# First-layer softmax sums turned and added up by VectorE instead of summed by TensorE

## The chip, the cores and the metric

The kernel runs on one core of one Trainium2 chip. A core has five engines that run side by side, each with its own queue: TensorE (PE in the profile; its weight loads are shown as PEld), VectorE (DVE), ScalarE (ACT), GpSimd (POOL) and SyncE (SP, which here issues DMA transfers). TensorE writes its results into PSUM, which holds eight banks of 128 partitions by 512 numbers of four bytes. The metric is the time of one execution on the device, in microseconds (us), as a median of several runs.

## The reference

Two layers of attention over images. The input x holds 8 images of 32 x 32 places with 512 channels. Each layer takes a group norm (32 groups of 16 channels), projects queries, keys and values, takes a softmax over the 1024 places of the image, multiplies by the values, projects the result, and adds it to x.

```python
# layer 0: 16 heads of 32 channels
qkv = xt @ w_qkv
attn = softmax(einsum('bhid,bhjd->bhij', q * 32 ** -0.5, k))
out = einsum('bhij,bhjd->bhid', attn, v) @ w_proj + b_proj
# layer 1: 4 heads of 128 channels, with relative positions
scores = (q @ k) / sqrt(128) + position_logits(q)
out = (softmax(scores) @ v) @ Wo
```

All of it is computed in four-byte floating point.

## The kernel before

**Layout.** An image is held with channels on the partitions, in four blocks of 128 channels by 1024 places. Scores are computed turned round: keys on the partitions, queries along the row. The softmax leaves out the subtraction of the maximum (a check of all sums at the end chooses a general path if that was not safe), so a head needs exp of the scores, the product of exp with the values, the sum of exp over the keys, and a division.

**The first layer's attention** (`attention_0`) works in steps. A step is named by (m, h, j): m is one of four blocks of four heads, h one of two halves of the queries (512), j one of eight blocks of 128 keys. `front` makes the scores of four heads (line 727) in the four-bank PSUM tile `ps` and lets ScalarE take exp (line 742) into one of the three slots of `e_room`, each 128 x 2048. `back`, one step later, multiplies by the values into the PSUM bank `acc` (line 753) and lets VectorE add the exp tile onto the first one of its group (line 765), so that after the eight steps of a group (m, h) one slot holds, for each of four heads, 128 partial sums for each query. Two slots take turns for exp; the third holds the running sum. When a new group begins, the slot of its first exp becomes the sum, and the old sum's slot joins the turn, so the exp of the third step of the new group writes over the old sum.

**The end of a group** (`finish`): four matmuls with a matrix of ones (line 775) add up the 128 partitions of each head's part and spread the sum over that head's 32 partitions, in the bank `acc`. `normalise` (lines 667 to 708) copies that to memory (ScalarE), turns it by blocks of 32 x 32 (VectorE, line 669), takes a reciprocal of 16 numbers per partition, notes the largest sum for the check, spreads the reciprocals back (line 704), and GpSimd multiplies the result q[m] by them (line 708).

**The second layer's attention** (`attention_1`) ends its groups in another way: `added_up` (lines 676 and 677) turns the 128 x 512 partial sums on VectorE and adds up blocks of 32, leaving 16 numbers per partition, and one small matmul with the constant matrix `fold` (line 895) adds the four partition groups and spreads the result.

**Projections** are 2 x 2 block products with seven multiplications (`seven`, line 341 by way of `by_columns`): products are summed into three PSUM tiles x, y and z, in the order x, y, x, y, z, y, z. VectorE reads the half-done y twice (`a`, line 431, and `b`, line 439), and the next product into y must wait for that. The tiles x, y, z come from the three banks tagged `bank`. Those banks also serve the second layer's scores and sums and the position logits (`pp`). The names in a profile carry the matrix: y_wo is the y of the output projection Wo of the second layer, y_q and y_k those of queries and keys, y_wp that of the first layer's projection.

**What sets the order.** A recording layer schedules the instructions when the program is built. The order on each engine is then fixed, and every engine works through its own queue; `issue_after` orders an instruction behind a given one on its engine. The Python generators set which work lies beside which: in image loop b, `side_by_side` draws the first layer's attention of image b step by step and spreads beside it the work of other images: the first layer's projection Wp of image b-1 (`after_0`), Wo of image b-2 woven with the group norm of image b-1 (`after_1`, `norm_1`), the second layer's projections with the position logits (`second`), the whole second attention of image b-1 between two steps, and the first layer's projections of image b+1. Every yield of `attention_0` counted as one step before. In loop 0 `attention_first` also draws the second unit of the value products. SyncE's queue carries weight slices, image blocks and outputs.

Of the kernel before, what the change touches and what calls it, by code (L numbers as in the profile page):

```python
# [9 lines left out]
F32 = mybir.dt.float32  # L10
# [17 lines left out]
def quick_path(  # L28
# [305 lines left out]

    added = [None]

    def by_columns(out, weights, moving, start, stop, open_sum=False):

        for g in range(P // 32):
            columns = slice(32 * g, 32 * g + 32)  # L340
            ins = nc.tensor.matmul(  # L341
                out[columns, :],
                weights[:, columns],
                moving,
                start=start,
                stop=stop,
                skip_group_check=open_sum,
            )
            if in_place[0]:
                tc.keep_in_program_order(ins)  # L350
        in_place[0] = False
# [65 lines left out]
    def seven(fs, u, rows, sink, name, hook=None):  # L417

        product = taken(fs, u, rows)
        x = bank(f"x_{name}")
        product(x, 0, True)
        p1 = snapshot("e1", f"p1_{name}")
        nc.scalar.copy(p1, x)
        yield HC
        y = bank(f"y_{name}")
        product(y, 5, True)
        a = snapshot("es1", f"a_{name}")  # L430
        reader[0] = begun[0] = nc.vector.tensor_add(a, y, p1)
        sink.early(p1, a)
        yield HC
        product(x, 1, False)
        sink.c11(x)
        yield HC
        product(y, 4, False)
        b = snapshot("es1", f"b_{name}")
        reader[0] = half_done[0] = nc.vector.tensor_add(b, y, p1)
        sink.middle(b)  # L440
        yield HC
        z = bank(f"z_{name}")
        product(z, 6, True)
        p7 = snapshot("e1", f"p7_{name}")
        nc.scalar.copy(p7, z)  # L445
        yield HC
        product(y, 2, False)
        sink.c12(y, p1)
        if hook is not None:
            hook()  # L450
        yield HC
        product(z, 3, False)
        sink.c21(z, a)
        sink.c22(b, p7)
        yield HC
# [14 lines left out]
    def five_last(fs, u, sink, name, p1):  # L470
        product = taken(fs, u, False)
        y = bank(f"y_{name}")
        product(y, 5, True)
        a = snapshot("es1", f"a_{name}")
        reader[0] = begun[0] = nc.vector.tensor_add(a, y, p1)
        sink.early(p1, a)
        yield HC
        product(y, 4, False)
        b = snapshot("es1", f"b_{name}")
        reader[0] = half_done[0] = nc.vector.tensor_add(b, y, p1)  # L480
        sink.middle(b)
        yield HC
        z = bank(f"z_{name}")
        product(z, 6, True)
        p7 = snapshot("e1", f"p7_{name}")
        nc.scalar.copy(p7, z)
        yield HC
        product(y, 2, False)
        sink.c12(y, p1)
        yield HC  # L490
        product(z, 3, False)
        sink.c21(z, a)
        sink.c22(b, p7)
        yield HC
# [75 lines left out]
    class Plain:  # L570
# [15 lines left out]
            nc.vector.tensor_add(self.dst[1][0], self.shape(y), self.shape(p1))  # L586

        def c21(self, z, a):
            nc.vector.tensor_add(self.dst[0][1], self.shape(z), self.shape(a))

        def c22(self, b, p7):
            s = self.shape
# [68 lines left out]
    def normalise(dst, acc_sums, name, engine=nc.gpsimd):  # L661

        su = mem.tile([P, NB], F32, tag="rec", name=f"su_{name}", bufs=2)
        nc.scalar.copy(su, acc_sums)
        turned = mem.tile([P, NB], F32, tag="rec", name=f"tu_{name}", bufs=2)
        nc.vector.transpose(turned, su)
        few = turned.rearrange("p (t c) -> p t c", c=32)[:, :, 0]  # L670
        multiply(dst, few, few, su, name, engine)

    def added_up(out, esum, name):

        turned = mem.tile([P, NB], F32, tag="rec", name=f"tu_{name}", bufs=2)
        nc.vector.transpose(turned, esum)
        nc.vector.tensor_reduce(
            out, turned.rearrange("p (t c) -> p t c", c=32), axis=AX.X, op=ALU.add
        )

    def few_tile(name, n=1):
        return mem.tile([P, n, NB // 32], F32, tag=f"few{n}", name=name, bufs=3 if n == 1 else 1)
# [31 lines left out]
    def attention_0(q, k, v, b, blocks=range(NT)):  # L714

        steps = [(m, h, j) for m in (0, 2, 1, 3) for h in range(NH) for j in blocks]
        state = {}

        def front(m, h, j):
            name = f"0_{b}_{m}_{h}_{j}"  # L720
            ps = psum.tile([P, HB, NB], F32, tag="ps", name=f"ps_{name}", bufs=1)
            for i in range(2):

                some = slice(64 * i, 64 * i + 64)
                for r in range(HB):
                    rows = slice(r * D0, (r + 1) * D0)
                    nc.tensor.matmul(  # L727
                        ps[some, r, :],
                        k[m][rows, j * P + 64 * i : j * P + 64 * i + 64],
                        q[m][rows, h * NB : (h + 1) * NB],  # L730
                        start=True,
                        stop=True,
                    )
            at = turn.pop(0)
            if j == blocks[0]:

                turn.append(sum_at[0])
                sum_at[0] = at
            else:
                turn.append(at)  # L740
            e = e_room[:, at]
            nc.scalar.activation(e, ps, AF.Exp, scale=D0 ** -0.5)  # L742
            return e

        def back(m, h, j, e):
            name = f"0_{b}_{m}_{h}_{j}"
            if j == blocks[0]:
                state["acc"] = psum.tile([P, NB], F32, tag="acc", name=f"acc_{name}", bufs=1)
                state["first"] = e
            acc = state["acc"]  # L750
            for r in range(HB):
                c0 = (m * HB + r) * D0
                nc.tensor.matmul(  # L753
                    acc[r * D0 : (r + 1) * D0, :],
                    v[:, j, c0 : c0 + D0],
                    e[:, r, :],
                    start=(j == blocks[0]),
                    stop=(j == blocks[-1]),
                )
            if j == blocks[1]:  # L760
                state["esum"] = state["first"]
            if j != blocks[0]:

                with tc.issue_after(reader[0].ins) if beside_norm[0] else nullcontext():
                    summed[0] = nc.vector.tensor_add(state["esum"], state["esum"], e)  # L765
            if j != blocks[-1]:
                return
            nc.scalar.copy(q[m][:, h * NB : (h + 1) * NB], acc)
            state["ended"] = (m, h, state["esum"])

        def finish(m, h, esum):
            name = f"0_{b}_{m}_{h}"
            su = psum.tile([P, NB], F32, tag="acc", name=f"sums_{name}", bufs=1)
            for r in range(HB):
                nc.tensor.matmul(
                    su[r * D0 : (r + 1) * D0, :],
                    ones,
                    esum[:, r, :],
                    start=True,
                    stop=True,  # L780
                )
            normalise(q[m][:, h * NB : (h + 1) * NB], su, name)

        pending = None
        for at in steps:
            if "ended" in state:
                finish(*state.pop("ended"))
            e = front(*at)
            if pending is not None:
                back(*pending)  # L790
            pending = (*at, e)
            yield 2
        back(*pending)
        yield 1
        finish(*state.pop("ended"))

    def position_logits(q, posT, b):

# [203 lines left out]
    def attention_first(st):  # L1002

        values = project_rows(st["xn"], WV0, st["v"], "v0_0", units=(1,))
        steps = attention_0(st["q"], st["k"], st["v"], 0, [0, 1, 4, 5, 2, 3, 6, 7])
        for at, cost in enumerate(steps):
            if at < NT // 2:
                for _ in range(2):
                    next(values, None)
            yield cost  # L1010
# [152 lines left out]
    def side_by_side(first, rest, total, alone=0):  # L1163


        steps = CC * NH * NT + 1 - alone
        done = 0
        at = -alone
        for _ in first:
            at += 1  # L1170
            while done * steps < total * at:
                cost = next(rest, None)
                if cost is None:
                    done = total * steps
                    break
                done += cost
        run(rest)
# [629 lines left out]
```

## Time and profile before

| what | us |
|---|---|
| median of 3 runs (3792.39 to 3792.98) | 3792.49 |
| the profiled execution | 3792.3 |
| its span, first to last instruction | 3790.5 |
| PE busy | 3764.2 (99%) |
| DVE busy | 2579.9 (68%) |
| ACT busy | 1689.2 (45%) |
| POOL busy | 651.4 (17%) |
| sums with ones, line 775, PE | 71.4 |
| e_room additions, line 765, DVE | 1074.6 (448 of 2399 ns) |
| granted TensorE clock | 0.999 of full |

In a row of groups stand the line, the engine, the operation, what is written and read by the program's names, the sizes and the count; then the busy time in us and the mean time of one in ns; then how long the engine stood idle just before, and what ended most of that. Busy time counts overlapping instructions once. Most matrix products appear as two records, and those of different column groups overlap, so 512 records of 596 ns are busy for only 71.4 us. A row of a timeline gives the start in us, the time from the first start to the last end in us, the instructions, and in brackets the idle time before and what ended it.

### The profile page before, as it was taken

To read this page: it belongs to the slowest core of one execution; us is meant where nothing else is said; L and a number is where in the kernel's file an instruction comes from. 1 tells how busy PE (TensorE), PEld (TensorE's weight loads), DVE (VectorE), ACT (ScalarE), POOL (GpSimd) and SP (SyncE) were. 2 spreads that over 40 slices of the span, in tenths; PEclk is the share of its full clock that TensorE was granted. 3 is DMA by queue.
4 is the path that set the end of the run, shared out by engine and by line. 5 is a ranking of instruction groups with operands and counts; after the bars stand their busy time and mean duration, and the time that the engine had idled before them with its cause. 6 is when DMAs were issued, how large, how long until landed. Compare 5 with 4: busy or idle time off the path is not lost. (4 is left out here: it accounts for less than half of the span.)

```text
span 3790.5 us, 79715 instructions
## 1 busy us (share of the span) xinstructions
PE 3764.2 (99%) x34478; PEld 1367.7 (36%) x34478; DVE 2579.9 (68%) x2974; ACT 1689.2 (45%) x1705; POOL 651.4 (17%) x397
## 2 busy tenths in 40 slices
PE   9999999999999999999999999999999999999998
PEld 4232244322443234432343323433234332334353
DVE  6778675686756867569665696656866569765555
ACT  3555543445434454344534445344453445553132
POOL 1342101131001310013101131011310113001201
PEclk9999999999999999999999999999999999999999
DMA  6122120232202312023120241103411033110321
GB/s 187 64 106 69 39 57 10 72 102 54 56 12 93 85 48 56 16 92 93 38 56 18 94 96 39 48 22 99 91 40 42 25 99 78 29 43 29 104 50 26
DMA packets 482982, 234.71 MB, mean 62 GB/s; under 512 B 269600, under 2 KB 461376, under 8 KB 481600
## 3 DMA queue, kind: packets, MB, share of 16 engines
q1 hardware_dynamic: 470992, 213.74, 20.6%
q0 software_dynamic: 2608, 13.70, 1.0%
q8 instruction: 273, 4.47, 0.5%
q10 hardware_dynamic: 9024, 2.10, 0.3%
q14 instruction: 85, 0.70, 0.1%
HBM read 170.72 MB, written 58.72 MB: 61 GB/s over the span
## 5 line engine op out<-in xcount | busy, mean ns | idle before, releaser
L765 DVE TENSOR_TENSOR e_room<-e_room 128x2048 f32<-128x2048 f32 x448 | 1074.6, 2399 | 403.3 <-ACT e_room L742 400.1
L742 ACT ACTIVATE e_room<-ps 128x2048 f32<-128x2048 f32 x512 | 961.9, 1879 | 788.6 <-PE ps L727 752.5
L853 ACT ACTIVATE e<-ps 128x512 f32<-128x512 f32 x512 | 306.0, 598 | 634.8 <-PE ps L851 594.2
L727 PE MATMUL ps<-q,k 32*64 32x512 f32 x8192 | 575.5, 613 | 0.2 <-ACT e_room L742 0.2
L753 PE MATMUL acc<-e_room,v 128*32 128x512 f32 x4096 | 551.0, 604 | 0.0
L850 PE MATMUL ps<-q,k 128*128 128x512 f32 x1024 | 529.6, 599 | 0.2 <-DVE posT L836 0.2
L862 PE MATMUL acc<-e,v 128*128 128x512 f32 x1024 | 521.8, 592 | 0.0
L873 DVE TENSOR_TENSOR es<-es,e 128x512 f32<-128x512 f32 x384 | 301.1, 784 | 292.8 <-ACT e L853 288.5
L708 POOL TENSOR_TENSOR q<-q,su 128x512 f32<-128x512 f32 x127 | 190.6, 1501 | 1488.1 <-DVE su L704 1443.6
L851 PE MATMUL ps<-posT,sel 128*128 128x512 f32 x512 | 406.7, 794 | 0.0
L850 PEld LDWEIGHTS ps<-q,k 128*128 128x128 f32 x1024 | 188.2, 190 | 225.1 <-issue 217.3
L727 PEld LDWEIGHTS ps<-q,k 32*64 32x64 f32 x8192 | 120.0, 129 | 389.1 <-issue 216.5
L862 PEld LDWEIGHTS acc<-e,v 128*128 128x128 f32 x1024 | 193.1, 189 | 146.8 <-issue 105.2
L753 PEld LDWEIGHTS acc<-e_room,v 128*32 128x32 f32 x4096 | 81.9, 108 | 411.4 <-issue 364.1
L851 PEld LDWEIGHTS ps<-posT,sel 128*128 128x128 f32 x512 | 97.3, 190 | 122.5 <-issue 122.5
L836 DVE TENSOR_TENSOR posT<-pp,posT 32x512 fp32r<-32x512 f32 x128 | 111.8, 874 | 31.9 <-ACT posT L831 30.6
L593 POOL TENSOR_TENSOR k<-b_k,p_k 128x512 f32<-128x512 f32 x32 | 50.4, 1574 | 478.3 <-ACT p_k L445 467.6
L593 POOL TENSOR_TENSOR v<-b_v,p_v 128x512 f32<-128x512 f32 x32 | 51.5, 1609 | 436.4 <-ACT p_v L445 430.9
L831 ACT CAST posT<-pp 32x512 fp32r<-32x512 f32 x128 | 105.7, 826 | 46.0 <-PE pp L818 44.9
L593 POOL TENSOR_TENSOR q<-b_q,p_q 128x512 f32<-128x512 f32 x32 | 67.6, 2112 | 260.7 <-ACT p_q L445 260.7
L341 PE MATMUL y_v<-w_v,f_xn 128*32 128x256 f32 x1536 | 100.8, 381 | 0.0
L341 PE MATMUL y_k<-f_xn,w_k 128*32 128x512 f32 x768 | 100.7, 594 | 0.0
(223 smaller groups left out, 4384.0 us busy)
## 6 DMA issues: line engine op xcount, KB each, us to landing
w_qkv<-ws_qkv SPq DMA_DIRECT2D x168, 128.0 KB, 2.4
d<-x0T SPq DMA_DIRECT2D x32, 512.0 KB, 3.1
x1T<-d SPq DMA_DIRECT2D x32, 512.0 KB, 5.4
d<-x1T SPq DMA_DIRECT2D x32, 512.0 KB, 3.6
x2T<-d SPq DMA_DIRECT2D x32, 512.0 KB, 6.2
w_qkv<-in_L_conv_w_qkv SPq DMA_DIRECT2D x126, 128.0 KB, 2.2
out<-ot SPq DMA_DIRECT2D x240, 64.0 KB, 2.0
xs<-in_x SPq DMA_DIRECT2D x224, 64.0 KB, 2.5
```

Of the source, the lines that this page charges most:

```text
L341: ins = nc.tensor.matmul(out[columns, :], weights[:, columns], moving, start=start, stop=stop, skip_group_check=open_sum,)
L593: nc.gpsimd.tensor_tensor(self.dst[1][1], s(b), s(p7), op=ALU.add)
L708: engine.tensor_tensor(dst, dst, su, op=ALU.mult)
L727: nc.tensor.matmul(ps[some, r, :], k[m][rows, j * P + 64 * i : j * P + 64 * i + 64], q[m][rows, h * NB : (h + 1) * NB], start=True, stop=True,
L742: nc.scalar.activation(e, ps, AF.Exp, scale=D0 ** -0.5)
L753: nc.tensor.matmul(acc[r * D0 : (r + 1) * D0, :], v[:, j, c0 : c0 + D0], e[:, r, :], start=(j == blocks[0]), stop=(j == blocks[-1]),)
L765: summed[0] = nc.vector.tensor_add(state["esum"], state["esum"], e)
L850: nc.tensor.matmul(ps, k[h][:, keys], q[:, h, queries], start=True, stop=False)
L851: nc.tensor.matmul(ps, sel_flat[:, keys], posT[:, h, queries], start=False, stop=True)
L853: nc.scalar.activation(e, ps, AF.Exp, scale=1.0 / math.sqrt(D1))
L862: nc.tensor.matmul(acc, v[:, j, h * D1 : (h + 1) * D1], e, start=(j == 0), stop=(j == NT - 1),)
L873: added[0] = nc.vector.tensor_add(state["esum"], state["esum"], e)
```

## The change

The group end of the first layer takes the second layer's way, for all groups of an image but the last. `finish` becomes a generator. It is created at the end of the step in which the group's last `back` ran. In the second half of that step VectorE turns and adds up heads 0 and 1 (`added_up`), in the second half of the next step heads 2 and 3. After two more half-step calls four small matmuls with `fold` combine them in a bank tagged `bank`, and `normalise_few` does the rest; it has no copy by ScalarE and no turning. The last group of each image keeps the matmuls with ones and `normalise`.

The turns are ordered behind `calm[0]`: the last recorded VectorE instruction that read a half-done y (`a` or `b`), or a Plain output from z (`c21`). `attention_0` now yields twice per step, each for half of a step, and `side_by_side` counts by half; `attention_first` draws its value products at every second yield.

```diff
-        reader[0] = begun[0] = nc.vector.tensor_add(a, y, p1)
+        reader[0] = begun[0] = calm[0] = nc.vector.tensor_add(a, y, p1)
...
-        reader[0] = half_done[0] = nc.vector.tensor_add(b, y, p1)
+        reader[0] = half_done[0] = calm[0] = nc.vector.tensor_add(b, y, p1)
...
-            nc.vector.tensor_add(self.dst[0][1], self.shape(z), self.shape(a))
+            calm[0] = nc.vector.tensor_add(self.dst[0][1], self.shape(z), self.shape(a))
...
         def finish(m, h, esum):
             name = f"0_{b}_{m}_{h}"
-            su = psum.tile([P, NB], F32, tag="acc", name=f"sums_{name}", bufs=1)
+            dst = q[m][:, h * NB : (h + 1) * NB]
+            if (m, h) == steps[-1][:2]:
+                su = psum.tile([P, NB], F32, tag="acc", name=f"sums_{name}", bufs=1)
+                for r in range(HB):
+                    nc.tensor.matmul(
+                        su[r * D0 : (r + 1) * D0, :], ones, esum[:, r, :], start=True, stop=True
+                    )
+                normalise(dst, su, name)
+                return
+            few = few_tile(f"fw_{name}", HB)
+            for r in range(HB):
+                if r % 2 == 0:
+                    yield
+                with tc.issue_after(calm[0].ins):
+                    added_up(few[:, r, :], esum[:, r, :], f"{name}_{r}")
+            yield
+            yield
+            su = bank(f"sums_{name}")[:, : NB // 32]
             for r in range(HB):
                 nc.tensor.matmul(
-                    su[r * D0 : (r + 1) * D0, :],
-                    ones,
-                    esum[:, r, :],
-                    start=True,
-                    stop=True,
+                    su[r * D0 : (r + 1) * D0, :], fold[:, 0, :], few[:, r, :], start=True, stop=True
                 )
-            normalise(q[m][:, h * NB : (h + 1) * NB], su, name)
+            normalise_few(dst, su, name)
 
         pending = None
+        ending = iter(())
         for at in steps:
-            if "ended" in state:
-                finish(*state.pop("ended"))
             e = front(*at)
             if pending is not None:
                 back(*pending)
             pending = (*at, e)
-            yield 2
+            if "ended" in state:
+                ending = finish(*state.pop("ended"))
+                next(ending)
+            yield 1
+            next(ending, None)
+            yield 1
         back(*pending)
-        yield 1
-        finish(*state.pop("ended"))
+        yield 2
+        run(finish(*state.pop("ended")))
...
-            if at < NT // 2:
+            if at < NT and at % 2:
...
-        for _ in first:
-            at += 1
+        for cost in first:
+            at += cost / 2
```

More of the change, by code (lines that the diff above doesn't have):

```diff
@@ L335, in quick_path @@
     added = [None]
+    calm = [None]
     def by_columns(out, weights, moving, start, stop, open_sum=False):
@@ L474, in five_last @@
         a = snapshot("es1", f"a_{name}")
-        reader[0] = begun[0] = nc.vector.tensor_add(a, y, p1)
+        reader[0] = begun[0] = calm[0] = nc.vector.tensor_add(a, y, p1)
         sink.early(p1, a)
@@ L479, in five_last @@
         b = snapshot("es1", f"b_{name}")
-        reader[0] = half_done[0] = nc.vector.tensor_add(b, y, p1)
+        reader[0] = half_done[0] = calm[0] = nc.vector.tensor_add(b, y, p1)
         sink.middle(b)
```

## The prediction

> **What bounds the kernel now.** I read the page's busy times first, then the groups of instructions by line, the waits, the stage windows, and last the timelines of the stretch that the windows point at.
>
> The page's first part, and TensorE's own entry in the table of waits (longest in total, times, longest):
>
> ```profile
> PE 3764.2 (99%) x34478; PEld 1367.7 (36%) x34478; DVE 2579.9 (68%) x2974; ACT 1689.2 (45%) x1705; POOL 651.4 (17%) x397
> ...
> PE y_q L341 <- DVE a_q L431: 0.6, 1, 0.6
> ```
>
> TensorE (PE) is busy 99% of the span, and no engine keeps it waiting for long. What leaves TensorE shortens the program, as long as nothing new makes it wait. VectorE (DVE) has 32% free on average. The groups that the change touches or resembles:
>
> ```profile
> L775 PE MATMUL sums<-e_room,ones 128*32 128x512 f32 x512 | 71.4, 596 | 2.4 <-ACT q L768 2.0 <-DVE e_room L765 0.4
> L669 DVE STREAM_TRANSPOSE tu<-su 128x512 f32<-128x512 f32 x64 | 45.2, 706 | 54.4 <-ACT su L667 51.4 <-POOL q L708 2.9
> L676 DVE STREAM_TRANSPOSE tu<-es 128x512 f32<-128x512 f32 x64 | 45.1, 705 | 1.7
> L677 DVE TENSOR_REDUCE fw<-tu 128x16 f32<-128x512 f32 x64 | 43.8, 684 | 2.0
> L895 PE MATMUL sums<-fw,fold 128*128 128x16 f32 x128 | 19.5, 227 | 0.0
> ```
>
> The average hides where VectorE is full. Windows of 10 us (columns: length, PE, weight loads, DVE, ACT, POOL busy, clock, DMA share, GB/s), in image loop 3:
>
> ```profile
> 1270.00:1280.00 10.00, 10.00 (x108) 2.50 (x104) 9.90 (x17) 5.31 (x6) 2.12 (x2) 1.00 0.45 164
> ...
> 1310.00:1320.00 10.00, 10.00 (x108) 2.60 (x104) 9.86 (x13) 4.94 (x4) 3.27 (x2) 1.00 0.51 115
> 1320.00:1330.00 10.00, 9.89 (x104) 2.24 (x96) 8.89 (x9) 4.34 (x3) 0.00 (x0) 1.00 0.60 117
> 1330.00:1340.00 10.00, 10.00 (x116) 2.57 (x112) 6.55 (x5) 4.80 (x4) 1.95 (x1) 1.00 0.51 97
> ```
>
> From 1263 to 1325 VectorE is busy 60.8 of 62 us. The same stretch comes back near 800, 1730, 2200 and 2660, longer near 3130, and shorter near 340. It is where Wp's, the norm's and Wo's element work falls beside the first layer's first two groups. Its end, in the timelines of PE and DVE:
>
> ```profile
> 1270.92 1.05 PE L775 MATMUL sums<-e_room,ones 128*32 128x512 f32 x8
> 1271.90 1.11 PE L727 MATMUL ps<-q,k 32*64 32x512 f32 x16
> ...
> 1322.55 1.90 PE L341 MATMUL x_q<-x1T,w_q 128*32 128x512 f32 x16
> 1324.56 1.92 PE L341 MATMUL y_q<-f_xn,w_q 128*32 128x512 f32 x16
> ...
> 1321.66 2.24 DVE L765 TENSOR_TENSOR e_room<-e_room 128x2048 f32<-128x2048 f32 x1
> 1323.83 0.67 DVE L431 TENSOR_TENSOR a_q<-y_q,p_q 128x512 f32<-128x512 f32 x1
> 1324.43 2.27 DVE L765 TENSOR_TENSOR e_room<-e_room 128x2048 f32<-128x2048 f32 x1
> ```
>
> A set of 16 product records takes 1.72 us start to start, so the y_q product was due at 1324.27. It starts at 1324.56, after a_q, which reads the bank it adds to: VectorE's slack is already used up there. The sums take 0.98 us of TensorE (1270.92 to 1271.90).
>
> [...] a_q sits behind an e_room addition while its operands have long been there, and TensorE stops.
>
> **The change, part by part.** 56 of 64 finishes change, seven per image.
>
> *TensorE, removed:* 56 x 0.98 = 54.9 us. *Added:* eight fold records of 16 columns in four column groups. In the second layer a fold's two records take 0.14 us to the next matmul (1503.97 to 1504.11), which then takes 0.08 longer: 0.22 is the low end. Eight weight loads of 110 ns, none hidden, give 0.9. I take 0.3, near the low end, because the eight sums loads now cover one another (14.1 us busy in all, where 512 x 109 ns would be 56). [...] Net -0.68 each, -38.1 us if nothing waits.
>
> *ScalarE, removed:* 56 copies of 0.59 us. They lie beside TensorE's products; removing them is worth only the 2.0 us that sums waited for L768.
>
> *VectorE, added:* four transposes and four reductions per finish. Three transposes in a row take 1.88 us (1296.54), so 0.63 each; an operation of 0.69 lets the next start after 0.60, so a reduction takes 0.60. 4 x 0.63 + 4 x 0.60 = 4.92. *Removed:* one transpose, 0.63. Net +4.3, x 56 = 240 us: VectorE goes to about 2820 us, 74%. Most of it is covered by TensorE's products; not in the stretch.
>
> *The stretch.* By the built order of the changed kernel, between a_wp of the second unit and a_q, both groups' eight transposes and reductions each stand ahead of a_q, all other VectorE work is the same, and one reciprocal chain (1315.02 to 1316.04, 1.02 us) moves behind a_q. Nothing queued there can be skipped. So a_q moves by 2 x 4.92 - (0.62 + 0.71) for the old transposes - 1.02 - 0.59 idle used up (0.28 and 0.31, at 1282.98 and 1291.68) = +6.9 us, and TensorE waits for it: first at the wo products' a_wo and its banks, in all until the y_q product. TensorE's own saving of 1.4 us vanishes into that wait. +6.9 for each of image loops 2 to 6. In loop 7 both chains stay ahead of a_q: 9.84 - 1.43 - 1.47 idle = +7.0, then -1.0 for the third finish. In loop 1 only one group falls in: 4.92 - 0.62 - 0.87 idle = 3.4 at a_q, less 0.9 of slack, +2.6.
>
> *Two lighter places.* Group (2,1) ends beside a position stage (1395 to 1407, VectorE nearly full): exp must wait for the last transpose, and the fold takes the bank of z_k, whose reader stands behind an e_room addition. Following the queue by hand from 1395.68, with 4.92 added and the old chain's 1.86 taken off, TensorE waits 0.3 + 0.3 + 1.0 us: +0.8 net. Group (1,0) ends just ahead of the second layer's attention (1442): v's readers move 1.9 us and hold its first score bank, then its third e: waits of 1.4 and 0.8, +1.0 net. Both in loops 1 to 6. If VectorE has more slack than I see, both are -0.7; if less, twice as much.
>
> *Elsewhere* (groups (2,0), (1,1), (3,0)) VectorE is 50 to 70% busy; after the final e_room addition it has no addition to make for one step, and eight instructions fit. -0.68 each. The e_room slot must be free by the exp of the third step; the last transpose is some 1.5 us ahead of it there.
>
> *Moved:* reciprocal, check, spread and POOL's multiplication come about two steps later; POOL idled 1444 us ahead of it, and the output is read a group later at the earliest. SP's queue has five block loads one place later: covered by DMA queues busy about a fifth of the time; uncovered, some 2 us each. The first image's value products and the half counts issue the same work half a step later: nothing.
>
> *Sum against the profiled 3792.3 us (span 3790.5):* loop 0: 7 x -0.68, +2.5 for stretches at 94 to 96% (70 to 90, 150 to 160) = -2.3. Loop 1: +2.6 + 1.8 - 4 x 0.68 = +1.7. Loops 2 to 6: 6.9 + 0.8 + 1.0 - 3 x 0.68 = +6.7, x 5 = 33.5. Loop 7: 7.0 - 1.0 - 0.5 = +5.5. In all +38: 3830 us. The runs' median, 3792.49, is the profiled time within 0.2.
>
> **The rivals.**
> *VectorE's work hides (faster).* Over the whole span it fits: 240 us into 1210 idle. Then 38 + 2 us come off: 3752. It decides from the point where a_q is no later than 1324.3 less TensorE's lead; against it, the queue order and the stall already there. 0.08.
> *The two sides cancel.* If only the six stretches cost (about 41 us) and all 44 others gain 0.68 (-30), with a fold at 0.22 or VectorE's instructions a tenth cheaper: 3792 to 3800. 0.06 for within 0.2%.
> *The fold's bank becomes a second bound.* A fold takes one of three banks from its start to VectorE's check. If that costs 1 us at half of the 44 finishes outside the stretch beyond what I count, 3850 to 3860. For it: both ends hang on a full queue. Against it: in the light places the bank was free for several products. 0.12.
> That the change doesn't do what it says is excluded by the built order: 448 transposes and reductions on VectorE, 224 fold matmuls on TensorE.
>
> **How the numbers follow.** Forecast 0.74, bank 0.12, faster 0.08, same 0.06. A difference of 0.2% (7.6 us) is about what a measurement of this kernel can tell from none. Slower 0.86. Range: low end the stretches alone with little loss elsewhere, 3798; high end the forecast with the lighter places doubled and half the bank rival, 3856.
>
> **What would show it.** Right: PE idle before L341 and at the stretch's ends released by DVE a_wo, a_q and x2T, near 8 us per stretch; windows there with PE at 85 to 90% and DVE at 97% or more; the period between such stretches growing from 467 to about 474 us; elsewhere PE at 100%. Wrong: PE still 100% in the stretches (faster), or waits at the folds or score matmuls outside them (bank).

## The result, and the profile after

| kernel | median us | runs | ratio to before, 95% interval |
|---|---|---|---|
| before | 3792.61 | 4, 3792.39 to 3792.98 | |
| changed | 3835.01 | 4, 3831.09 to 3836.99 | 1.0110 (1.0097 to 1.0123) |

The change costs 42.4 us; the profiled execution, 3836.99 us with a span of 3835.2, costs 44.7. The forecast was 3830. The first part of the changed kernel's page:

```profile
PE 3742.5 (98%) x34478; PEld 1361.3 (35%) x34478; DVE 2772.7 (72%) x3366; ACT 1655.3 (43%) x1649; POOL 651.0 (17%) x397
```

TensorE's busy time fell by 21.7 us (its slow stretches, below, count as busy) and the program is 44.7 us longer, so its idle time grew from 26.3 to 92.7 us. The groups that the change touches:

```profile
L679 DVE TENSOR_REDUCE fw<-tu 128x16 f32<-128x512 f32 x288 | 183.2, 664 | 2.2
L678 DVE STREAM_TRANSPOSE tu<-e_room 128x512 f32<-128x512 f32 x224 | 145.9, 685 | 1.7 <-POOL q L710 0.9
```

And TensorE's waits; before, the longest in this table for a reader of half-done sums was 0.6 us:

```profile
PE y_q L343 <- DVE a_q L433: 15.3, 7, 2.8
PE ps L729 <- ACT e_room L744: 10.0, 13, 1.7
PE y_wo L343 <- DVE a_wo L433: 9.0, 10, 0.9
PE sums L794 <- DVE fw L679: 6.7, 7, 2.0
PE y_wo L343 <- DVE x2T L610: 6.1, 6, 1.1
...
PE sums L794 <- DVE k L591: 4.3, 5, 0.9
```

The first, third and fifth are the predicted stretch. Its windows of 10 us in image loop 3 (same columns as before; the loop begins 13.7 us later here):

```profile
1290.00:1300.00 10.00, 9.14 (x106) 2.30 (x104) 9.96 (x16) 3.76 (x2) 4.78 (x3) 1.00 0.63 207
...
1310.00:1320.00 10.00, 7.93 (x84) 1.64 (x72) 10.00 (x12) 4.24 (x3) 3.28 (x2) 1.00 0.40 61
...
1330.00:1340.00 10.00, 9.01 (x96) 2.21 (x92) 9.96 (x13) 3.94 (x4) 0.00 (x0) 1.00 0.33 67
1340.00:1350.00 10.00, 7.21 (x85) 1.95 (x84) 9.97 (x12) 3.09 (x4) 1.29 (x1) 1.00 0.68 125
```

VectorE (the third busy figure) is full, and TensorE (the first) falls to 72 to 91% in these four windows; in those between it stays full. The end of the stretch, in the timelines of PE and DVE:

```profile
1339.16 1.90 PE L343 MATMUL x_q<-x1T,w_q 128*32 128x512 f32 x16
1340.88 0.23 PE L794 MATMUL sums<-fw,fold 128*32 128x16 f32 x8
1343.90 1.92 PE L343 MATMUL y_q<-f_xn,w_q 128*32 128x512 f32 x16 [2.79 <-DVE a_q L433]
...
1341.00 2.25 DVE L767 TENSOR_TENSOR e_room<-e_room 128x2048 f32<-128x2048 f32 x1
1343.17 0.68 DVE L433 TENSOR_TENSOR a_q<-y_q,p_q 128x512 f32<-128x512 f32 x1
```

TensorE has the fold behind it at 1341.11 and waits 2.79 us for a_q, which stands in VectorE's queue behind an e_room addition. The same place in loop 2, on PE, and then windows of 1 us there, whose third last column is the granted clock:

```profile
868.24 0.23 PE L794 MATMUL sums<-fw,fold 128*32 128x16 f32 x8
871.27 3.39 PE L343 MATMUL y_q<-f_xn,w_q 128*32 128x512 f32 x16 [2.79 <-DVE a_q L433]
```

```profile
870.00:871.00 1.00, 0.00 (x0) 0.00 (x0) 1.00 (x2) 0.00 (x0) 0.00 (x0) 0.93 0.81 118
871.00:872.00 1.00, 0.73 (x4) 0.20 (x8) 1.00 (x2) 0.00 (x0) 0.00 (x0) 0.50 0.82 122
872.00:873.00 1.00, 1.00 (x12) 0.22 (x8) 1.00 (x1) 0.00 (x0) 0.00 (x0) 0.50 0.83 124
873.00:874.00 1.00, 1.00 (x12) 0.18 (x4) 0.97 (x5) 0.00 (x0) 0.00 (x0) 0.50 0.69 134
874.00:875.00 1.00, 1.00 (x16) 0.23 (x16) 0.69 (x2) 0.00 (x0) 0.44 (x1) 0.86 0.85 238
```

The wait is the same, but the product behind it lasts 3.39 us instead of 1.92: the granted clock stood at half for about 3.4 us, and 0.07 + 3 x 0.5 + 0.14 = 1.7 us of work were lost. Before, the clock is 1.00 from 30 us to 3780. After, it falls in eight such places: three in image loop 0 (160 to 240 us), one each in loops 2, 5 and 6, two in loop 7. Their deficits in the 10-us windows add up to 13.6 us. The prediction had no such term.

From the starts of the first exp of each image loop (line 742 before, 744 after, in ScalarE's timeline), the loss by loop of the profiled execution:

| stage | predicted us | measured us | of it half-speed clock |
|---|---|---|---|
| ahead of loop 0 | 0 | +0.6 | |
| loop 0 | -2.3 | +5.7 | 5.1 |
| loop 1 | +1.7 | +1.4 | |
| loops 2 to 6 | +33.5 | +26.8 | 5.1 |
| loop 7 and the rest | +5.5 | +10.2 | 3.4 |
| sum | +38 | +44.7 | 13.6 |

The border between the first two loops hides something. Before, 28 records of the x_wp product run in loop 0 (from 297.85 us on); in the changed kernel none runs before 316.49, so that they fall into loop 1's first group, which grows by 2.66 us. Run 1, below, shows the same 2.66 with no new work on VectorE. The work has only crossed the border: put back, loop 0 lost 8.4 us, and loop 1 gained 1.3.

### The profile page after: what moved, and what is told of

The parts are those of the page before. It is cut to its first block, busy times and chain, and to the rows that moved or that the text cites. A ratio compares the mean times of both kernels' runs of the same rounds, so it can differ in the third digit from the quotient of the medians.

```text
span 3835.2 us, 80064 instructions
## 1 busy us (share of the span) xinstructions
PE 3742.5 (98%) x34478; PEld 1361.3 (35%) x34478; DVE 2772.7 (72%) x3366; ACT 1655.3 (43%) x1649; POOL 651.0 (17%) x397
## 4 chain that ended last, share of the span: by engine, by line
PE 82%; DVE 13%; issue 2%; ACT 1%; DMA 1%; POOL 0%; SPq 0%; DVEq 0%; ACTq 0%; POOLq 0%
PE acc L881 11%; PE ps L869 11%; PE ps L729 11%; PE acc L755 10%; DVE e_room L767 5%; PE y_q L343 4%; PE y_v L343 4%; PE y_k L343 4%; PE ps L870 3%; PE z_q L343 3%; PE x_k L343 3%; PE x_v L343 3%; PE z_v L343 2%; PE x_q L343 2%; PE z_k L343 2%; PE y_wp L343 2%
## 5 line engine op out<-in xcount | busy, mean ns | idle before, releaser
L767 DVE TENSOR_TENSOR e_room<-e_room 128x2048 f32<-128x2048 f32 x448 | 1046.9, 2337 | 350.5 <-ACT e_room L744 347.8
L710 POOL TENSOR_TENSOR q<-q,su 128x512 f32<-128x512 f32 x127 | 210.4, 1657 | 1492.6 <-DVE su L706 1438.8
L679 DVE TENSOR_REDUCE fw<-tu 128x16 f32<-128x512 f32 x288 | 183.2, 664 | 2.2
L678 DVE STREAM_TRANSPOSE tu<-e_room 128x512 f32<-128x512 f32 x224 | 145.9, 685 | 1.7 <-POOL q L710 0.9
L595 POOL TENSOR_TENSOR q<-b_q,p_q 128x512 f32<-128x512 f32 x32 | 56.0, 1750 | 383.3 <-ACT p_q L447 361.2
L343 PE MATMUL y_q<-f_xn,w_q 128*32 128x512 f32 x768 | 94.8, 613 | 16.8 <-DVE a_q L433 15.3
```

The lines of the kernel that those rows point to most:

```text
L343: ins = nc.tensor.matmul(out[columns, :], weights[:, columns], moving, start=start, stop=stop, skip_group_check=open_sum,)
L679: nc.vector.tensor_reduce(out, turned.rearrange("p (t c) -> p t c", c=32), axis=AX.X, op=ALU.add)
L710: engine.tensor_tensor(dst, dst, su, op=ALU.mult)
```

## The experiments

Shifts "at a finish" below are taken the same way: the time from the first exp of one group to that of the next, less the same time before. A group's finish falls into the next group's time.

**1. The folds without VectorE's work.**

```diff
-            few = few_tile(f"fw_{name}", HB)
...          (the turns and additions of four heads go too)
+            few = const_few
...          (const_few is written once, at the start)
```

> The change with its folds, in the same places and banks, but without VectorE's turns and additions of the first layer: the folds read a constant written once, so the sums of 56 groups are left out. Theory (VectorE's queue is the whole cost): nothing waits, each finish saves TensorE what the groups without a wait show in the profile of the changed kernel, 0.8 us; 3792.5 - 56 x 0.8 = 3748, between 3745 and 3752, with the clock at 1.00 throughout image loops 1 to 6. With the prediction's 0.68 it would be 3754. Rival (the bank that the fold takes is a second bound, 1 us at half of the 44 finishes outside the stretch): about 3770, with waits at the products after the folds.

Measured: 3753.63 us, ratio 0.9896 (0.9879 to 0.9912). The range was 3745 to 3752. All but VectorE's turns and additions is as in the changed kernel, so they, with the half-speed clock that they bring, cost 3835.0 - 3753.6 = 81 us there. At finishes without a wait the shift is -0.80 to -0.82 us, so a fold costs 0.98 - 0.80 = 0.18. Two things kept it from 3748. Among its waits are these:

```profile
PE y_wo L343 <- DVE a_wo L433: 4.4, 5, 0.9
...
PE z_k L343 <- issue: 3.2, 1, 3.2
```

In the stretch VectorE is the limit even without new work, so of two savings of 0.8 only 0.83 in all is left. And in loop 7 the finish of (2,1) loses 4.1 us although VectorE does nothing new. The wait for z_k is the changed kernel's too, there on PE and DVE:

```profile
3294.53 0.23 PE L794 MATMUL sums<-fw,fold 128*32 128x16 f32 x8
3297.95 3.49 PE L343 MATMUL z_k<-x1T,w_k 128*32 128x512 f32 x16 [3.19 <-issue]
...
3294.39 3.46 DVE L855 TENSOR_TENSOR posT<-pp,posT 32x512 fp32r<-32x512 f32 x4 [0.94 <-ACT posT L850]
```

The trace names no releaser, but z_k starts 0.10 us after the last read of pp (3297.85); the likely reading is that the fold has taken the free bank and z_k must wait for that of pp. Then z_k itself runs at half speed (3.49 us; the granted clock is 0.89 and 0.94 in the windows from 3290 to 3310). Runs 9 and 10 end this one group in the old way: the wait is gone and the shift is 0.0 and 0.1. That is the bank rival, in one place, for some 5 us.

**2. VectorE's work without the folds.**

```diff
+            if late is not None:
+                old_finish(*late)
+                late = None
             e = front(*at)
...
-            su = bank(f"sums_{name}")[:, : NB // 32]
...          (fold and normalise_few go too; old_finish holds the matmuls with ones)
```

> The kernel before with VectorE's turns and additions put in beside it, in the changed kernel's places; the sums still come from the matmuls with ones and the results of the turns are not used. Theory (VectorE's queue): in the stretches the end is VectorE's, so removing nothing from TensorE changes nothing there and the old turns come on top: about 8 us each in loops 2 to 6, 10 in loop 7, 4 in loop 1, 1 to 2.5 us more per loop at the two lighter places, and 0 to 10 us of half-speed clock: 3855 to 3885. Rival (the fold and its bank are the cost): 3792 to 3800.

Measured: 3930.67 us, ratio 1.0365 (1.0348 to 1.0383), far above what the theory gave. Its longest waits:

```profile
PE acc L755 <- ACT su L669: 46.5, 25, 3.2
...
PE y_q L343 <- DVE a_q L433: 17.3, 7, 3.3
```

The y_q waits are as in the changed kernel (15.3 us there). The first line is this experiment's own: the sums with ones lie in the bank `acc` until ScalarE has copied them into one of the two `rec` tiles, and the turns now use these two as well. So the run measures a collision that the change doesn't have. Against the rival (3792 to 3800) speak its y_q waits, which are there with no fold of the first layer in the kernel; its total says nothing.

**3. The first two groups of loops 1 to 7 in the old way.**

```diff
+        def turned_way(m, h):
+            return (m, h) != (3, 1) and not (b > 0 and m == 0)
...
-            if (m, h) == steps[-1][:2]:
+            if not turned_way(m, h):
```

> The change, but the first two groups of image loops 1 to 7, (0,0) and (0,1), end in the old way with ones. Theory: the stretches cost nothing any more. From the profile of the changed kernel that takes off 5.7 us in each of loops 2 to 6 (2.74 + 2.94), 4.5 of half-speed clock in three of them, 7.3 in loop 7 and about 3 in loop 1: 3835 - 43 = 3792, between 3787 and 3798. Rival (cost spread over all folds by their bank): 14 of 56 finishes give back a quarter of 90 us less 11: 3823.

Measured: 3789.91 us, ratio 0.9994 (0.9985 to 1.0003). As the theory had it: 14 of 56 finishes carry nearly the whole loss. Of the 47 us between the two profiled executions 42 lie in loops 1 to 7; 4.8 lie in loop 0, where nothing was edited (run 8 says why). The shift at both places is 0.0 in loops 2 to 7, and the waits for a_wo and the five of 2.8 us for a_q are gone from its table.

**4. The new way in 18 calm places alone.**

```diff
+            return (m, h) in ((2, 0), (1, 1), (3, 0)) and 0 < b < B - 1
```

> The new way only for groups (2,0), (1,1) and (3,0) of image loops 1 to 6, 18 of 64; all others end in the old way. Theory: no wait there, 18 x -0.8 = -14.4: 3778, between 3776 and 3782, the clock 1.00 in all loops. Rival (bank): 1 us lost at half of them, 3787 or more.

Measured: 3779.20 us, ratio 0.9964 (0.9950 to 0.9978): 13.6 us for 18 finishes, against the kernel before of the same series, 3792.80. All 18 shift by -0.74 to -0.86, all others by 0.1 or less, but for the last stretch of the program (+0.9). The bank costs nothing there.

**5. Half of VectorE's work.**

```diff
+        half = turned[:, : NB // 2]
+        nc.vector.transpose(half, esum[:, : NB // 2])
+        nc.vector.tensor_reduce(
+            out, half.rearrange("p (t c) -> p t c", c=16), axis=AX.X, op=ALU.add
+        )
...
-                    added_up(few[:, r, :], esum[:, r, :], f"{name}_{r}")
+                    half_added(few[:, r, :], esum[:, r, :], f"{name}_{r}")
```

> The change with VectorE's turns and additions over 256 of the 512 queries only (half the sums are left out); every instruction is there, each about half as long, 0.3 us instead of 0.6. Theory (each us of VectorE's queue in the stretch is a us at the y_q product): 9.84 becomes about 5.0 for the two groups, so a stretch of loops 2 to 6 costs 5.7 - 4.8 = +0.9 us instead of 5.7 to 7.2; the half-speed intervals and loop 0's waits for the folds' operands go with it: 3775 to 3790. If the number of instructions or the banks mattered and not VectorE's time, it stays above 3815.

Measured: 3782.34 us, ratio 0.9972 (0.9961 to 0.9983). A stretch of loops 2 to 6 costs 0.87 + 0.78 = 1.65 us, so with none, half and all of VectorE's work it costs -0.8, +1.7 and +5.7. From half to all, VectorE has 8 x 0.27 + 8 x 0.26 = 4.2 us more of it to do for the two groups (0.34 us a turn and 0.32 a reduction at half width, start to start, against 0.61 and 0.58), and the stretch is 4.0 longer: a us of VectorE's queue is nearly a us of the program there. From none to half it is less, 2.5 us for 5.3, as the kernel with none has some slack.

**6. Without the order behind the readers.**

```diff
-                with tc.issue_after(calm[0].ins):
-                    added_up(few[:, r, :], esum[:, r, :], f"{name}_{r}")
+                added_up(few[:, r, :], esum[:, r, :], f"{name}_{r}")
```

> The change without the ordering of the turns behind the readers of half-done sums; only VectorE's order changes (the turns of one half step come ahead of b_q, b_k, b_v, a_k and of position reads, 2.5 us each). Theory: readers 2.5 us later keep y's next product waiting where less than that lies between, 3 to 5 places per image: 3837 to 3855. Rival: TensorE has a product of another tile in between, no difference: 3832 to 3838.

Measured: 3814.08 us, ratio 1.0054 (1.0039 to 1.0069). Neither theory: it is 21 us faster than the change. In the profiled executions 4.9 us of the difference lie in loop 0, mostly half-speed intervals that did not occur in this one (see run 8); loop 7 is equal, though it has two such intervals more; 16.2 lie in loops 2 to 6, and these are the order. The stretch is unchanged (2.7 and 2.9 us at its two finishes), but in loops 2 to 6 the finish of (2,1) goes from +0.6 to +0.8 down to -0.7 to -0.9, and that of (1,0) from +0.45 to -1.34: 3.3 us per loop, 16 us in the five. Why, VectorE's timeline shows. The changed kernel, behind the finish of (2,1) in loop 3:

```profile
1406.51 0.68 DVE L433 TENSOR_TENSOR a_k<-y_k,p_k 128x512 f32<-128x512 f32 x1
1412.49 0.69 DVE L441 TENSOR_TENSOR b_k<-y_k,p_k 128x512 f32<-128x512 f32 x1 [5.30 <-PE y_k L343]
1414.12 1.74 DVE L855 TENSOR_TENSOR posT<-pp,posT 32x512 fp32r<-32x512 f32 x2 [0.94 <-ACT posT L850]
1415.89 1.30 DVE L678 STREAM_TRANSPOSE tu<-e_room 128x512 f32<-128x512 f32 x2
...
1427.63 0.68 DVE L591 TENSOR_TENSOR k<-z_k,a_k 128x512 f32<-128x512 f32 x1
```

And without the order:

```profile
1397.97 0.68 DVE L433 TENSOR_TENSOR a_k<-y_k,p_k 128x512 f32<-128x512 f32 x1
1398.57 1.29 DVE L678 STREAM_TRANSPOSE tu<-e_room 128x512 f32<-128x512 f32 x2
1399.79 1.24 DVE L679 TENSOR_REDUCE fw<-tu 128x16 f32<-128x512 f32 x2
1400.94 1.29 DVE L678 STREAM_TRANSPOSE tu<-e_room 128x512 f32<-128x512 f32 x2
1402.16 1.24 DVE L679 TENSOR_REDUCE fw<-tu 128x16 f32<-128x512 f32 x2
1404.03 0.69 DVE L441 TENSOR_TENSOR b_k<-y_k,p_k 128x512 f32<-128x512 f32 x1 [0.64 <-PE y_k L343]
```

Ordered behind b_k, the turns sit in a queue whose head waits 5.30 us for TensorE's y_k, and VectorE does nothing. Unordered, all of 4.75 us of turns and additions fits into that gap and is free, and b_k still waits for TensorE. In the changed kernel the turns come nearly 9 us later, VectorE works through to 1431, the reader of z_k comes at 1427.63, and the fold waits for its bank (PE; the first table of waits has five such):

```profile
1428.37 0.26 PE L794 MATMUL sums<-fw,fold 128*32 128x16 f32 x8 [0.86 <-DVE k L591]
```

At (1,0) the head of the queue is b_v, ahead of which VectorE stands idle for 3.38 us in the changed kernel; without the order all four turns and two of the four additions stand ahead of b_v and fit in there.

**7. The folds two steps later.** The group end is drawn once per step, so each added `yield` is a whole step; the change's own "two more half-step calls" are two steps as well, and the "one step" of the expectations below means these two yields.

```diff
             yield
             yield
+            yield
+            yield
             su = bank(f"sums_{name}")[:, : NB // 32]
```

> The change with the folds one whole step later. Theory on loop 0: its steps last 3.8 us, VectorE's turns and additions 4.9, so the folds come too early there (6.7 us of waits for fw) and draw half-speed intervals (5 us); both go. The wait of the fold for z_k's bank, 0.9 in each of loops 2 to 6, goes too or moves. The stretches stay, since a_q's place in VectorE's queue is the same: 3835 - 12 - 4 = 3819, between 3812 and 3828. Rival (loop 0's loss is VectorE's load, wherever the fold stands): 3832 to 3838.

Measured: 3839.53 us, ratio 1.0122 (1.0107 to 1.0138). Wrong in the sum, right on loop 0: by the table's count that loop takes 5.1 us less than before, where the change takes 5.7 more and, in the profiles without half-speed clock there (those of 3, 6 and 8), 0.9 to 1.1 more. (The 2.7 us that crossed the border are in all of these.) What it pays with, in its waits:

```profile
PE x_wo L343 <- DVE x2T L610: 16.1, 5, 3.2
...
PE sums L796 <- DVE posT L857: 9.6, 6, 1.7
```

In loops 2 to 6 the stretch goes from 5.7 us to 8.0 to 8.7, with two half-speed intervals in each (mean clock of the run 0.994), some 3 us; without them it would be no longer than the changed kernel's. The finish of (2,0) goes from -0.8 to +1.0, and x_wo now stands still for up to 3.2 us before a bank is read out by an x2T addition. The fold's bank is cheap or dear by what stands behind it on TensorE.

**8. Matmuls of no use in the gaps.**

```diff
+            for r in range(sets * HB):      # sets: 2 at (0,1) in loops 2 to 6, 4 and 3 in loop 7
+                nc.tensor.matmul(room[r % HB * D0 : (r % HB + 1) * D0, 32:], ones, k[m][:, 32:NB],
+                                 start=True, stop=True)
```

> The change with matmuls of no use (into the unused columns of the fold's bank) ahead of the fold in front of the longest waits: 1.84 us in each of loops 2 to 6 ahead of the y_q wait of 2.79, 3.7 and 2.8 us in loop 7 ahead of those of 4.25 and 3.19. Theory (a long wait makes the clock fall to half for some 3.4 us, 1.7 us lost each time): TensorE is kept busy, the clock stays at 1.00 in loops 2 to 7, and although seven places get work added nothing is lost for it: 8 us less where the profile of the changed kernel has five such intervals, 3825 to 3830. Rival (the slow matmuls after a wait are another thing, and the clock column follows it): no gain, 3833 to 3842.

Measured: 3824.84 us, ratio 1.0086 (1.0072 to 1.0099). Loop 2, on PE:

```profile
862.60 1.79 PE L800 MATMUL sums<-k,ones 128*32 128x480 f32 x16
864.21 0.23 PE L808 MATMUL sums<-fw,fold 128*32 128x16 f32 x8
865.62 1.92 PE L343 MATMUL y_q<-f_xn,w_q 128*32 128x512 f32 x16 [1.18 <-DVE a_q L433]
```

This is just below the range of 3825 to 3830. The product behind the wait lasts 1.92 us, not 3.39, and the clock is 1.00 throughout all image loops. Nor is it one lucky execution: the mean clock of all five is 0.998 to 0.999, that of the changed kernel's four 0.995 to 0.996. Where the changed kernel had half-speed intervals, loops 2, 5 and 6 are each about 1.5 us shorter, and loop 7 up to its last group is 2.8 shorter with seven sets of useless matmuls in it. A further 4.7 us came off in loop 0, where nothing was edited: there the three intervals simply did not occur in this execution, nor in those profiled for 3 and 6. So the intervals come and go from one execution to the next, 1.7 us each, and the changed kernel's spread of 5.9 us between its runs, where before has 0.6 (in the longer series with the other runs 1.8 to 3.0), is about what three or four of them would make.

**9 and 10. Only where it pays.** The new way without the order behind the readers; in loops 1 to 7 not for (0,0), (0,1), (3,1), in loop 7 not for (2,1). In loop 0, run 9 takes it for four groups, run 10 for all seven with the folds two steps later. The fence shows run 10.

```diff
-                with tc.issue_after(calm[0].ins):
...
+            return (m, h) != (3, 1) and (
+                True if b == 0 else m != 0 and (b, m, h) != (B - 1, 2, 1)
+            )
...
+            if b == 0:
+                yield
+                yield
```

> The new way without the ordering behind the readers, and only where the runs so far showed a gain: image loops 1 to 7 all groups but (0,0), (0,1), (3,1), and in loop 7 not (2,1), whose fold takes z_k's bank; in loop 0 only (0,0), (0,1), (1,1), (3,0). Theory (order and full queue are the whole cost, and they act place by place, so the places can be added up): from the shifts in the run without the ordering, 5 x -4.5 in loops 2 to 6, -4.1 in loop 1, -4.2 in loop 0, -4.0 in loop 7: 3792.7 - 34.8 = 3758, between 3754 and 3763, the clock at 1.00 in all loops. Rival (leaving the stretches alone moves the waits elsewhere): 3770 or more.

> The same, but in loop 0 all seven groups the new way, with the fold one step later there. Theory (in loop 0 the fold came too early for VectorE, and later folds found their operands ready in the run with later folds): loop 0 gives -5.1 or more instead of -4.2: 3757, between 3753 and 3762. If three more turns fill VectorE's queue in loop 0, 3760 to 3765.

Measured: 3765.48 us for 9, ratio 0.9928 (0.9914 to 0.9942), and 3760.18 us for 10, ratio 0.9914 (0.9900 to 0.9927). Run 10 is the fastest kernel here that computes all the sums. In loops 2 to 6 both gain 4.4 to 4.6 each, as added up from the single places. Run 9 misses its range, mostly in loop 0: -1.3 by the table's count instead of -4.2, and with the 2.1 us that crossed the border here put back, +0.9; TensorE still waits 3.9 us there for the folds' operands. In run 10 loop 0 gives -5.6, put back -2.9.

## Why the prediction was right and wrong

The sign, the place and most of the mechanism held; that 3830 lies so near 3835 is in part luck: loops 2 to 6 were forecast 11.8 us too dear, and 13.6 us of half-speed clock were not forecast at all.

- **The stretch: right, mis-sized.** Predicted +6.9 us each in loops 2 to 6; +5.7 without half-speed clock, and VectorE full as foretold. TensorE's waits there come to 6.7 us per stretch (2.8 for a_q, 1.8 for a_wo, 1.1 for x2T, 1.0 for an exp), not near 8, and the loops' period is 471 to 473 us. From its e_room addition at 1268.47 to a_q at 1323.83 the kernel before needs 55.36 us; the changed one, 1282.14 to 1343.17, 61.03. Part of the 1.2 between is the price of a finish: 4.74 us start to start (1286.80 to 1289.17 is half of one) instead of 4.92. The rest lies in small changes of other VectorE instructions, both ways (one e_room addition 3.07 to 2.28, one x2T addition 0.68 to 1.77), which were not tested. Runs 3 and 5 show cause and slope.
- **TensorE's saving: right, a little small.** -0.80 per finish, not -0.68: the term was the fold, taken at 0.3 and measured at 0.18. In the trace the eight records of a fold, spread over four column groups, start within 0.05 us, 6 to 9 ns apart (so at 1678.21). Over 56 finishes, -6.7 us.
- **VectorE's added work: a little large.** Predicted +240 us busy, measured +193. The e_room additions, which the change does not touch, came down from 1074.6 to 1046.9 us (2337 ns each instead of 2399); no run says why. Another 10 us are the cheaper finish.
- **The two lighter places: size near, reason wrong.** Predicted +0.8 and +1.0; +0.7 and +0.45. The step put it on VectorE's load. VectorE was idle for 5.30 and 3.38 us there; the order behind b_k and b_v made the work late. Run 6: with the order gone both places gain. The step counted what is queued ahead of the turns and never asked whether the queue's head would be waiting. In loop 1 both finishes gained 0.75 where +1.8 in all was predicted.
- **Loop 0: wrong.** Predicted -2.3 in all, with +2.5 lost in full stretches; without half-speed clock it came to +3.3, the work that crossed the border put back. The folds waited 6.7 us for their own operands. A step takes 3.8 us there, the turns and additions 4.7, and they start behind the group's last e_room addition. In three of the seven groups half of the fold even stands in the very step in which the turns begin (fold at 160.36, first turn at 158.43); in the later loops it stands three steps on, and "eight instructions fit" was right only for those. Run 7 confirms it: these waits come down to 1.4 us. Loop 1's forecast (+1.7 against a measured +1.4) was met by luck: put back it is -1.3, since its two lighter places gained.
- **The bank rival: true at single places.** Not at the 18 calm ones (run 4), but in loop 7 (runs 1, 9 and 10, some 5 us); and run 7 moves the folds and gets new waits at the fold (9.6 us for posT) and at the product behind it (16.1 us for x2T), which are waits for a bank to be read out.
- **The missing term.** Half-speed clock after waits, 13.6 us in the profiled execution: eight intervals of 3.4 us at a granted clock of 0.50, 1.7 us lost in each. The prediction did not ask about the clock, since before there was no wait to ask about. Where it fell in loops 2, 5 and 6, TensorE had waited 2.79 us for a_q; in loops 3 and 4 it waited as long and the clock stayed at 1.00. Run 8 shows the cause: with 1.61 us of that gap filled and 1.18 left, the clock stays at 1.00.

Added up against the forecast: loops 2 to 6 without half-speed clock -11.8, loop 0 +5.6 and loop 1 -3.0 (with the work at their border put back), loop 7 +0.8 and its end and the start +1.0, half-speed clock +13.6: +6.2, and 38.4 + 6.2 = 44.6. "VectorE's work hides" fell at the point it named: a_q is later than TensorE's need.

## What to carry to other kernels

Cost an added instruction by the place in the queue where it is issued, and look at what the head of that queue waits for there: the same 4.75 us were free in one place, cost 5.7 us for two groups in another, and cost 1.5 to 1.8 us in a third only because they had been ordered behind a reader that was itself waiting. When a change brings gaps to a TensorE that had none, look at the granted clock too: here it fell to half behind three of five gaps of 2.79 us, for 1.7 us each. And a change that loses as a whole may win by places: the shifts of single groups, read off against before, added up to within 0.1 us for each of loops 2 to 6 (-4.5 foretold, -4.4 to -4.6 measured), but not for loop 0 (-4.2 foretold, -1.3 measured).

## What the hardware showed beyond that

- After a gap of 2.79 us the granted clock fell to half for 3.4 us in three of five equal places (loops 2, 5 and 6: in the changed kernel, and in run 6, where the 10-us windows there show 0.83), which lost 1.7 us each; in the changed kernel's loops 3 and 4 it stayed at 1.00. In its loop 0 gaps of 1.52 and 0.36 us around a fold were followed by a product of 11 records that took 2.74 us (clock 0.83 from 190 to 200).
- In loops 2 and 6 the half-speed interval of the changed kernel begins inside the gap, 0.41 and 0.37 us ahead of the y_q product (870.86 and 2758.43); in loop 5 it begins 1.32 us after that product has started (2287.39). What decides which of the equal gaps is hit was not shown. In the profile of run 6 waits of the same 6.7 us for the folds' operands cost no clock in loop 0.
- A fold of eight small matmul records with their weight loads holds TensorE for 0.18 us: at 1428.37 it begins and the next scores follow at 1428.56.
- A turn of 256 columns takes 418 ns and of 512 columns 685, a reduction 391 and 664 (run 5 and the changed kernel): halving the width saved about 40%, not half.
